# One unit for four PSUM score banks, and two delays in place of one in a list scheduler

## The chip, the cores and the metric

The kernel runs on one core of a Trainium2 chip. The metric is the device time of one execution in microseconds (us). A core has the matrix engine TensorE (PE; its weight loads are shown apart as PEld), VectorE (DVE), ScalarE (ACT), GpSimd (POOL) and SyncE (SP). SBUF is the working memory. PE writes its results into PSUM, which has eight banks of 128 partitions by 512 fp32 values.

## The reference

Four residual layers work on x of shape (4, 1024, 128), all in fp32. Each layer has an attention half and a feed-forward half, and both are modulated in the same way:

```python
h = _layernorm(x, axis=-1) * (1 + ca) + sa
x = x + ga * attn(h)
h = _layernorm(x, axis=-1) * (1 + cb) + sb
x = x + gb * ffn(h)
```

L0 is a decayed linear attention and a mixture of eight experts. L1 is a stack of four blocks of causal linear attention with 16 heads of 8 features, each block followed by two layer norms and a GELU network of 128 to 512 to 128, and then a mixture of eight experts. L2 and L3 are delta-rule attentions, each followed by one expert network that is picked per batch row. The change concerns the inside of L1's attention, which in each chunk of 128 steps computes

```python
scores = jnp.einsum('bnchd,bnkhd->bnhck', q, k)
scores = jnp.where(mask, scores, 0.0)
intra = jnp.einsum('bnhck,bnkhe->bnche', scores, v)
```

and adds to `intra` a part from the running state of earlier chunks, divided by a running denominator.

## The kernel before

x and h lie in SBUF with the 128 features on the partitions and 4096 tokens along the free axis. Each stage goes over eight chunks n of 128 steps and handles the four batch rows b of a chunk together, so a usual tile is 128 by 512.

**Two orderings stand behind each other.** The kernel writes its work as Python generators ("chains"): one for the normalisation, one for the scores, one for the masks, one for the value product and so on. The class `Flow` runs all the chains of one stage as a list scheduler. A chain yields what it wants next: `take` (buffers of a kind), `wait` (a mark that another chain sets), `rank` (its priority), or `run` (so many us on such engines). `Flow.run` keeps a planned clock for each engine. It goes on with the chain of best rank among those that can start within 0.1 us of the earliest. After a `run`, the chain's planned time is the end of the work plus the constant `LATENCY`, 0.12 us, for every engine alike (line 186). Buffers come free at the planned time of the chain that gives them back. When a chain goes on, it emits its instructions; the order of emission is a priority. A second scheduler, that of the framework, then sets the final order of each engine's instructions. It can put other ready work between instructions that one chain emitted together. The order of each engine is fixed before the kernel runs, and semaphores make an engine wait where its next instruction's data isn't there. No planned time appears on the chip.

The planner runs in five stages: `l0`, `l1_attn`, `l1_ffn`, `l2_attn` and `l3_attn`. The feed-forward halves of L2 and L3 are written straight out.

**L1's attention.** For each block l and chunk n, `prep_step` makes q, k, v, the denominators and `qx`, four copies of q masked by head (L966, on ACT). Then, for each batch row b (4 blocks x 8 chunks x 4 rows = 128 groups):

- `scores` takes four banks of the kind `sp` and issues four fp32 matmuls, one for each group d of 32 partitions, in the order d = 2, 3, 1, 0. Each contracts over 32 rows only, and the four use different rows of the PE array. The matmul helper records all of them as L291.
- `mask_dve` multiplies three of the banks (d = 0, 1, 2) by the causal mask on DVE (L1005) into SBUF tiles `at`, and then gives the three banks back.
- `mask_act` copies the fourth bank (d = 3) on ACT (L1018), gives it back, and masks the copy on POOL (L1021).
- `values` multiplies the masked scores with v in 16 small matmuls (L1080) into the bank of kind `acc`.

`attn_out` divides (L1096), applies the output projection and adds the residual (L1104); the chain `tail` does the norms and the GELU network (L1127, L1133). The norm's steps are L501 to L534: transposes on PE, a copy on ACT, statistics and scaling on DVE (L510 to L518), and a power on POOL (L515).

The eight PSUM banks of this stage are three `ps`, one `acc` and four `sp`. The four `sp` banks are in stock as single buffers: `take("sp", 4)` waits for all of them and hands them out in the order in which they came free, so a bank's role (d = 0 to 3) can change from group to group. Two of the four carry the profile's name ps and two the name acc.

Of the kernel before, what the change touches and what calls it, by code (L numbers as in the profile page):

```python
# [12 lines left out]
ALU = mybir.AluOpType  # L13
# [97 lines left out]
class Flow:  # L111
# [1 line left out]

    LATENCY = 0.12
    TABLE = 1.3
    SLACK = 0.1

# [35 lines left out]
    def run(self, chains):  # L155
        live = [{"gen": g, "t": 0.0, "want": None, "rank": 0.0, "no": i} for i, g in enumerate(chains)]
        while live:
            ready, asked = [], set()
            for c in sorted(live, key=lambda c: (c["rank"], c["no"])):
                if c["want"] is not None and c["want"][0] == "take":  # L160
                    kind = c["want"][1][0]
                    if kind in asked:
                        continue
                    asked.add(kind)
                s = self._start(c)
                if s is not None:
                    ready.append((s, c))
            assert ready, [c["want"] for c in live]
            first = min(s for s, _ in ready)
            at, c = next((s, c) for s, c in ready if s <= first + self.SLACK)  # L170
            got = None
            if c["want"] is None or c["want"][0] == "rank":
                self.at = c["t"]
            elif c["want"][0] == "spawn":
                self.at = c["t"]
                live.append({"gen": c["want"][1], "t": c["t"], "want": None, "rank": c["rank"], "no": c["no"]})
            elif c["want"][0] == "run":
                end = c["t"]
                table, costs = c["want"][1]
                if table and table != self.table:  # L180
                    self.table = table
                    self.clock["ACT"] += self.TABLE
                for e, cost in costs.items():
                    self.clock[e] = max(self.clock[e], c["t"]) + cost
                    end = max(end, self.clock[e])
                c["t"] = self.at = end + self.LATENCY
            elif c["want"][0] == "wait":
                c["t"] = self.at = at
            else:
                kind, n = c["want"][1]  # L190
                self.free[kind].sort(key=lambda b: b.free_at)
                got = [self.free[kind].pop(0) for _ in range(n)]
                c["t"] = self.at = at
            try:
                c["want"] = c["gen"].send(got)
                if c["want"][0] == "rank":
                    c["rank"] = c["want"][1]
            except StopIteration:
                live.remove(c)
# [6 lines left out]
def take(kind, n=1):  # L206
    return ("take", (kind, n))


def one(kind):  # L210
    (b,) = yield take(kind)
    return b


def rank(r):

    return ("rank", r)
# [7 lines left out]
def wait(key):  # L225
    return ("wait", key)


def mm_len(n, m=P):

    return max(n, m) * 0.00167 + 0.01


def dve_len(n):
    return 0.16 + 0.00104 * n


def act_len(n):
    return 0.25 + 0.00083 * n


def pool_len(n):
    return 0.2 + 0.0021 * n
# [6 lines left out]
def adaln_stack_kernel(ctx: ExitStack, tc: tile.TileContext, a):  # L250
    nc = tc.nc
    V, S, G, PE = nc.vector, nc.scalar, nc.gpsimd, nc.tensor
# [37 lines left out]
    def mm(out, lhsT, rhs, start=True, stop=True):  # L290
        PE.matmul(out, lhsT, rhs, start=start, stop=stop)  # L291

    def rep(ap, n):

        return ap.unsqueeze(1).to_broadcast([ap.shape[0], n, ap.shape[1]])
# [5 lines left out]
    def v4(t):  # L301
        return t.rearrange("p (a b) -> p a b", b=P)
# [11 lines left out]
    def K(name):  # L314
        lo, hi = _CONST[name]
        return cst[:, lo:hi]
# [9 lines left out]
    ident, mu, sl = K("ident"), K("mu"), K("sl")  # L326
# [148 lines left out]
    def flow():  # L475
        return Flow()

    def banks():
        return [ps() for _ in range(6)] + [acc() for _ in range(2)]
# [4 lines left out]
    def norm_stock(fl, n):  # L484

        fl.stock("xt", [v4(norm_tile(("ln_xc", "ln_sq", "ln_xn")[i % 3])) for i in range(n)])
        for kind, shape in (("st", (P, 4, 6)), ("mv", (P, 4, 2)), ("ve", (P, 4)), ("rs", (P, 4))):
            stock(fl, kind, 2, shape)
# [4 lines left out]
    def norm(fl, src, dst, affine):  # L493
# [3 lines left out]
        pb = yield from one("ps")  # L497
        p = v4(pb.t)
        yield run(PE=4 * TR_LEN)
        for t in range(4):  # L500
            PE.transpose(p[:, t, :], src[:, t, :], ident)  # L501
        xt = xb.t
        yield run(ACT=act_len(512))
        S.copy(xt, p)
        fl.give(pb)
        st, mv = (yield from one("st")), (yield from one("mv"))
        ve, rs = (yield from one("ve")), (yield from one("rs"))
        yield run(DVE=4 * dve_len(P) + 5 * 0.16)
        for t in range(4):
            V.bn_stats(st.t[:, t, :], xt[:, t, :])  # L510
# [330 lines left out]
    def l1_attn():  # L841
        y4 = h4
        fl = flow()
# [3 lines left out]
        psum = banks()  # L847
        fl.stock("ps", psum[:3])
        fl.stock("acc", psum[3:4])
        fl.stock("sp", psum[4:])  # L850
        norm_stock(fl, 3)
        fl.stock("z", [v4(norm_tile(tag)) for tag in ("ln_xc", "ln_sq", "ln_xn")])
        stock(fl, "qx", 2, (P, 4, B, P))
# [124 lines left out]
        ats, nums = {}, {}  # L978
        every = [(l, n) for l in range(L1L) for n in range(NS)]

        def scores():

            for l, n in every:
                yield rank(l * NS + n)
                yield wait(("prep", l, n))
                k, qx = ready[l, n][1].t, ready[l, n][5].t
                for b in range(B):
                    sps = yield take("sp", 4)
                    yield run(PE=mm_len(512) + 0.2)
                    for d in (2, 3, 1, 0):  # L990
                        g = slice(32 * d, 32 * d + 32)
                        mm(v4(sps[d].t), k[g, b, :], qx[g, :, b, :])
                    ats[l, n, b] = [sps, None, None]
                    fl.mark(("scores", l, n, b))

        def mask_dve():
            for l, n in every:
                yield rank(l * NS + n)
                for b in range(B):
                    yield wait(("scores", l, n, b))  # L1000
                    sps = ats[l, n, b][0]
                    at3 = yield take("at", 3)
                    yield run(DVE=3 * dve_len(512))
                    for d in range(3):
                        V.tensor_tensor(at3[d].t, v4(sps[d].t), rep(mu, 4), ALU.mult)  # L1005
                    fl.give(*sps[:3])
                    ats[l, n, b][1] = at3
                    fl.mark(("dve", l, n, b))

        def mask_act():  # L1010
            for l, n in every:
                yield rank(l * NS + n)
                for b in range(B):
                    yield wait(("scores", l, n, b))
                    sp = ats[l, n, b][0][3]
                    a = yield from one("at")
                    yield run(ACT=act_len(512))
                    S.copy(a.t, v4(sp.t))  # L1018
                    fl.give(sp)
                    yield run(POOL=pool_len(512))  # L1020
                    G.tensor_tensor(a.t, a.t, rep(mu, 4), ALU.mult)  # L1021
                    ats[l, n, b][2] = a
                    fl.mark(("act", l, n, b))
# [92 lines left out]
        def tail_step(l, n, z):  # L1116
# [22 lines left out]
            if l == L1L - 1:  # L1139
# [4 lines left out]
                fl.give(o)  # L1144

        chains = [attn_out(), state(), values(), mask_dve(), mask_act(), scores()]
        fl.run(chains + [tail(0), tail(1), prep(0), prep(1), first()])

# [699 lines left out]
    for i, half in enumerate([l0, l1_attn, l1_ffn, l2_attn, l2_ffn, l3_attn, l3_ffn]):  # L1848
        if half is l1_attn:
            early.close()  # L1850
        if half is l2_attn:
            late.close()
        with tc.tile_pool(name=f"half{i}", bufs=2) as wk:
            half()
# [99 lines left out]
```

## Time and profile before

| what | value |
|---|---|
| median of 3 runs | 2646.59 us (2646.0 to 2646.84) |
| the profiled execution | 2641.42 us |
| its span, first to last instruction | 2639.7 us |
| mean granted TensorE clock | 0.929 |
| PE busy | 2308.3 us (87%) |
| DVE busy | 1333.0 us (50%) |
| ACT busy | 1154.9 us (44%) |
| POOL busy | 892.2 us (34%) |
| chain that ended last | PE 64%, DVE 17%, ACT 7%, POOL 6% |

A group of instructions in the profile is named by line, engine, operation and tiles as out<-in, followed by shapes and count. Behind the bar stand busy time, the mean duration of one in ns, and the idle time of the engine just before them with what ended it. An fp32 matmul stands in the profile as two instructions, each with its own weight load, so the counts of matmuls are twice those of the code. In a view of the waits, "A <- B: 30.7, 26, 2.1" says that A's engine stood idle for 30.7 us in all, 26 times, 2.1 us at most, until B had finished. The clock is the share of full speed that the chip granted to PE.

### The profile page before, as it was taken

To read this page: it belongs to the slowest core of one execution; us is meant where nothing else is said; L and a number is where in the kernel's file an instruction comes from. 1 tells how busy PE (TensorE), PEld (TensorE's weight loads), DVE (VectorE), ACT (ScalarE), POOL (GpSimd) and SP (SyncE) were. 2 spreads that over 40 slices of the span, in tenths; PEclk is the share of its full clock that TensorE was granted. 3 is DMA by queue.
4 is the path that set the end of the run, shared out by engine and by line. 5 is a ranking of instruction groups with operands and counts; after the bars stand their busy time and mean duration, and the time that the engine had idled before them with its cause. 6 is when DMAs were issued, how large, how long until landed. Compare 5 with 4: busy or idle time off the path is not lost.

```text
span 2639.7 us, 36709 instructions
## 1 busy us (share of the span) xinstructions
PE 2308.3 (87%) x13822; PEld 1387.7 (53%) x13822; DVE 1333.0 (50%) x3930; ACT 1154.9 (44%) x1964; POOL 892.2 (34%) x885
## 2 busy tenths in 40 slices
PE   5999989899999988889899869999799878788966
PEld 4654445454545444444454434444789633687842
DVE  5764346664654556655665554343654224455422
ACT  3653245445545444444444333333544226545424
POOL 1334444332433333333333222333634001544400
PEclk9999989998999989999999888999899879899978
DMA  5323300000000000000000001110000000000001
GB/s 209 88 67 99 101 0 1 1 1 1 1 1 1 1 1 1 1 1 1 1 1 1 1 33 64 65 65 33 1 1 1 1 26 7 1 1 1 1 1 48
DMA packets 29010, 61.46 MB, mean 23 GB/s; under 512 B 4256, under 2 KB 4512, under 8 KB 27808
## 3 DMA queue, kind: packets, MB, share of 16 engines
q1 hardware_dynamic: 27072, 53.86, 6.3%
q0 software_dynamic: 896, 3.16, 0.4%
q8 instruction: 109, 1.79, 0.3%
q10 hardware_dynamic: 864, 2.09, 0.2%
q14 instruction: 69, 0.57, 0.1%
HBM read 56.74 MB, written 2.36 MB: 22 GB/s over the span
## 4 chain that ended last, share of the span: by engine, by line
PE 64%; DVE 17%; ACT 7%; POOL 6%; issue 3%; DMA 1%; SPq 0%; ACTq 0%; POOLq 0%; DVEq 0%
PE ps L291 38%; PE acc L291 15%; PE ps L1080 4%; POOL rs L515 2%; DVE at L1005 2%; DVE st L510 2%; PE ps L526 2%; PE ps L501 1%; DVE ln_sq L518 1%; POOL at L1021 1%; DVE ln_xc L518 1%; DVE ve L513 1%; PE ps L1258 1%; DVE x L455 1%; DVE ln_xn L518 1%
## 5 line engine op out<-in xcount | busy, mean ns | idle before, releaser
L291 PE MATMUL ps<-h,w 128*128 128x512 f32 x760 | 380.3, 616 | 33.3 <-DVE ln_xc L1104 8.7
L291 PEld LDWEIGHTS ps<-h,w 128*128 128x128 f32 x760 | 140.5, 197 | 191.1 <-issue 133.8
L1021 POOL TENSOR_TENSOR at<-at,cst 128x512 f32<-128x512 f32 x128 | 162.7, 1271 | 202.8 <-ACT at L1018 198.3
L291 PE MATMUL acc<-qx,k 32*128 32x512 f32 x512 | 209.7, 669 | 6.9 <-DVE at L1005 6.9
L291 PE MATMUL acc<-fu,w 128*128 128x512 f32 x432 | 210.6, 607 | 0.9 <-POOL fu L818 0.9
L515 POOL TENSOR_TENSOR rs<-ve,mhalf 128x4 f32<-128x4 f32 x120 | 122.9, 1024 | 252.6 <-DVE ve L513 230.1
L291 PE MATMUL ps<-qx,k 32*128 32x512 f32 x512 | 198.7, 671 | 7.2 <-DVE at L1005 7.2
L1080 PE MATMUL ps<-at,vz 128*32 128x128 f32 x4096 | 168.2, 292 | 36.8 <-POOL at L1021 30.7
L1235 POOL TENSOR_TENSOR lv<-cl,cst 128x512 f32<-128x512 f32 x112 | 141.2, 1273 | 164.0 <-PE ps L291 92.3
L1080 PEld LDWEIGHTS ps<-at,vz 128*32 128x32 f32 x4096 | 116.4, 116 | 111.7 <-issue 45.0
L1005 DVE TENSOR_TENSOR at<-acc,cst 128x512 f32<-128x512 f32 x190 | 126.9, 681 | 74.2 <-PE acc L291 46.1
L1005 DVE TENSOR_TENSOR at<-ps,cst 128x512 f32<-128x512 f32 x194 | 129.2, 680 | 56.6 <-PE acc L291 29.1
L1127 ACT ACTIVATE fu<-ps,cols 128x512 f32<-128x512 f32 x128 | 87.9, 687 | 156.3 <-PE ps L291 155.5
L818 POOL TENSOR_TENSOR fu<-fu,gate 128x512 f32<-128x512 f32 x88 | 110.9, 1266 | 131.0 <-DVE fu L814 114.9
L291 PE MATMUL ps<-fu,w 128*128 128x512 f32 x256 | 150.3, 672 | 5.3 <-ACT fu L1127 5.2
L291 PE MATMUL ps<-y,w 128*128 128x512 f32 x256 | 145.5, 652 | 8.5 <-DVE tmp L1040 2.1
L1203 ACT ACTIVATE fu<-ps,cols 128x512 f32<-128x512 f32 x128 | 88.0, 687 | 131.8 <-PE ps L291 128.5
L1207 POOL TENSOR_TENSOR fu<-fu,gate 128x512 f32<-128x512 f32 x64 | 83.4, 1310 | 166.7 <-ACT fu L1203 143.8
L291 PEld LDWEIGHTS acc<-fu,w 128*128 128x128 f32 x432 | 81.8, 195 | 95.2 <-issue 86.8
L1206 DVE TENSOR_TENSOR fu<-fu,gate 128x512 f32<-128x512 f32 x64 | 51.9, 823 | 119.7 <-ACT fu L1203 118.1
L291 PE MATMUL ps<-iU,lv 128*128 128x128 f32 x608 | 93.0, 301 | 20.4 <-DVE iU L1269 16.9
L291 PEld LDWEIGHTS ps<-iU,lv 128*128 128x128 f32 x608 | 83.2, 211 | 28.8 <-issue 12.1
(489 smaller groups left out, 4686.2 us busy)
## 6 DMA issues: line engine op xcount, KB each, us to landing
gate<-gd SPq DMA_DIRECT2D x96, 256.0 KB
w<-in_w SPq DMA_DIRECT2D x7, 1024.0 KB
gate<-gd SPq DMA_DIRECT2D x16, 224.0 KB
gate<-gd SPq DMA_DIRECT2D x16, 192.0 KB
gate<-gd SPq DMA_DIRECT2D x16, 160.0 KB
x<-in_x SPq DMA_DIRECT2D x8, 256.0 KB
gate<-gd SPq DMA_DIRECT2D x16, 128.0 KB
out_x<-x SPq DMA_DIRECT2D x8, 256.0 KB
```

What stands on the lines that cost most here:

```text
L291: PE.matmul(out, lhsT, rhs, start=start, stop=stop)
L510: V.bn_stats(st.t[:, t, :], xt[:, t, :])
L515: G.tensor_tensor(rs.t, ve.t, mhalf, ALU.pow)
L518: V.tensor_scalar(xt[:, t, :], xt[:, t, :], mv.t[:, t, 0:1], rs.t[:, t : t + 1], ALU.subtract, ALU.mult)
L818: G.tensor_tensor(u.t, u.t, g.t, ALU.mult)
L1005: V.tensor_tensor(at3[d].t, v4(sps[d].t), rep(mu, 4), ALU.mult)
L1021: G.tensor_tensor(a.t, a.t, rep(mu, 4), ALU.mult)
L1080: PE.matmul(num[g, b, :], vz[:, b, s * P + 32 * d : s * P + 32 * d + 32], at4[d].t[:, s, :], start=n == 0 and s == 0 and b == 0, stop=s == ...
L1127: S.activation(flat(u.t), pb.t, AF.Gelu, bias=C(f"l1_b1{l}", f))
L1203: S.activation(u.t, pa.t, AF.Relu, bias=C("l1f_b1", 2 * e + j))
L1207: G.tensor_tensor(us[1].t, us[1].t, g.t, ALU.mult)
L1235: G.tensor_tensor(b.t, cl.t, rep(lvl[:, k * P : (k + 1) * P], B), ALU.mult)
```

## The change

There are two parts.

In `Flow`, the delay behind a `run` is no longer 0.12 us for all. It becomes 0.10 us, and 0.16 us more when PE was among the engines of the `run`. This holds in all five planned stages.

In `l1_attn`, the four score banks become one unit. They are in stock as one buffer that holds a list of the four banks, so bank d always has role d. The unit is free again when both readers are through: the new function `through` notes the first and gives the unit back at the second. The planned cost of a score group grows by 0.1 us. Before the four score matmuls a matmul of one column is issued, which writes into one column of bank 3 from the rows 96 to 127 (d = 3); the full matmul of d = 3 overwrites that column later. No DMA is added, and the output is computed as before.

```diff
-    LATENCY = 0.12
+    LATENCY = 0.1
+    DRAIN = 0.16
...
-                c["t"] = self.at = end + self.LATENCY
+                c["t"] = self.at = end + self.LATENCY + (self.DRAIN if "PE" in costs else 0.0)
...
-        fl.stock("sp", psum[4:])
+        fl.stock("sp", [psum[4:]])
...
-                    sps = yield take("sp", 4)
-                    yield run(PE=mm_len(512) + 0.2)
+                    quad = yield from one("sp")
+                    yield run(PE=mm_len(512) + 0.3)
+
+
+                    mm(v4(quad.t[3])[:, 0, 0:1], k[96:, b, :], qx[96:, 0, b, 0:1])
                     for d in (2, 3, 1, 0):
                         g = slice(32 * d, 32 * d + 32)
-                        mm(v4(sps[d].t), k[g, b, :], qx[g, :, b, :])
-                    ats[l, n, b] = [sps, None, None]
+                        mm(v4(quad.t[d]), k[g, b, :], qx[g, :, b, :])
+                    ats[l, n, b] = [quad, None, None]
                     fl.mark(("scores", l, n, b))
+
+        def through(quad):
+
+            if half_read.pop(quad, None) is None:
+                half_read[quad] = fl.at
+                return
+            fl.give(quad)
+
+        half_read = {}
...
-                        V.tensor_tensor(at3[d].t, v4(sps[d].t), rep(mu, 4), ALU.mult)
-                    fl.give(*sps[:3])
+                        V.tensor_tensor(at3[d].t, v4(quad.t[d]), rep(mu, 4), ALU.mult)
+                    through(quad)
...
-                    S.copy(a.t, v4(sp.t))
-                    fl.give(sp)
+                    S.copy(a.t, v4(quad.t[3]))
+                    through(quad)
```

More of the change, by code (lines that the diff above doesn't have):

```diff
@@ L1000, in mask_dve @@
                     yield wait(("scores", l, n, b))
-                    sps = ats[l, n, b][0]
+                    quad = ats[l, n, b][0]
                     at3 = yield take("at", 3)
@@ L1014, in mask_act @@
                     yield wait(("scores", l, n, b))
-                    sp = ats[l, n, b][0][3]
+                    quad = ats[l, n, b][0]
                     a = yield from one("at")
                     yield run(ACT=act_len(512))
-                    S.copy(a.t, v4(sp.t))
-                    fl.give(sp)
+                    S.copy(a.t, v4(quad.t[3]))
+                    through(quad)
                     yield run(POOL=pool_len(512))
```

## The prediction

> **What bounds the kernel now.** I read the table by stretches first, cut where the stages begin and end.
>
> ```profile
> 45.00:366.00 321.00, 309.99 (x1144) 169.39 (x1142) 164.16 (x570) 134.02 (x255) 139.51 (x113) 0.99 0.25 73
> 366.00:1557.00 1191.00, 1060.96 (x7928) 567.09 (x7928) 693.98 (x1875) 550.04 (x830) 405.00 (x455) 0.93 0.00 1
> 1557.00:1840.00 283.00, 264.15 (x688) 119.37 (x688) 116.66 (x340) 110.64 (x189) 90.99 (x71) 0.95 0.18 60
> 1840.00:2077.00 237.00, 211.05 (x1628) 197.41 (x1628) 128.88 (x386) 107.05 (x249) 106.17 (x86) 0.94 0.00 1
> 2212.00:2510.00 298.00, 254.38 (x1795) 219.82 (x1794) 147.20 (x487) 156.77 (x294) 136.39 (x141) 0.93 0.00 1
> ```
>
> Columns: stretch and length, then busy time of PE, PEld, DVE, ACT, POOL, granted clock, DMA. The second row is the linear-attention stage: 1191 of 2640 us, PE busy for 1061 (89%), DVE 58%, ACT 46%, and no DMA. PE is the bound and is idle for 130 us. The other planned stages leave 11, 19, 26 and 44 us idle. So the change can gain by giving PE less to do or by taking PE's waits away. The timeline of PE in this stage shows the first:
>
> ```profile
> 1018.83 0.70 PE L291 MATMUL ps<-qx,k 32*128 32x512 f32 x2
> 1018.85 0.70 PE L291 MATMUL acc<-qx,k 32*128 32x512 f32 x2
> 1019.37 0.59 PE L291 MATMUL ps<-qx,k 32*128 32x512 f32 x2
> 1019.38 0.59 PE L291 MATMUL acc<-qx,k 32*128 32x512 f32 x2
> 1019.90 1.13 PE L291 MATMUL ps<-y,w 128*128 128x512 f32 x2
> ...
> 1024.57 1.12 PE L291 MATMUL acc<-qx,k 32*128 32x512 f32 x2
> 1025.62 1.13 PE L291 MATMUL ps<-fu,w 128*128 128x512 f32 x2
> 1026.67 0.69 PE L291 MATMUL ps<-qx,k 32*128 32x512 f32 x1
> ...
> 1039.57 0.96 PE L291 MATMUL ps<-cst,tmp 128*128 128x16 f32 x8
> 1040.38 0.64 PE L526 MATMUL ps<-cst,ln_sq 128*128 128x128 f32 x4
> ```
>
> Each fp32 matmul is two passes. Four score matmuls in four row groups run side by side: from 1018.83 to 1019.90, 1.07 us for all four. At 1024.57 one stands alone and takes 1.05 us as well, and its three partners come at 1026.67 for another 1.05. A divided group pays again for each part. The waits of PE in this stage show the second, the idle time:
>
> ```profile
> PE ps L1080 <- POOL at L1021: 30.7, 26, 2.1
> PE ps L291 <- DVE ln_xc L1104: 8.7, 5, 2.5
> PE ps L291 <- DVE ln_xn L1104: 8.7, 4, 2.5
> PE ps L291 <- DVE ln_sq L1104: 8.2, 4, 2.5
> PE ps L291 <- DVE at L1005: 7.2, 7, 3.8
> PE acc L291 <- DVE at L1005: 6.9, 13, 3.1
> PE ps L291 <- ACT fu L1127: 5.2, 8, 1.9
> ```
>
> The columns are total, times, longest. The masked scores that come over ACT and POOL are the largest (30.7); the bank that L1104 reads after the output projection holds up the next user three times over (25.6); the score banks cost 14.1.
>
> **The change, part by part.** The sum is made against the profiled execution (2641.4 us, span 2639.7); the median of the runs is 2646.6, and I carry the difference in us over to it. All counts of order come from the two built programs.
>
> *Score groups in one piece.* Before, the 128 groups lie in 212 stretches (58 groups whole, 48 as one and three). After, without the one-column matmuls, they lie in 191 (85 whole). 21 fewer x 1.05 us = **-22 us**, all on PE. The value matmuls (L1080), which use column groups, go from 156 stretches to 148; stretches of 8, 16, 24 and 32 passes take 0.36, 0.57, 0.79 and 1.01 us from start to start, so 0.14 us is the price of an extra one: **-1 us**.
>
> *The added matmul.* 128 matmuls of one column, two passes each, with two weight loads, in the row group of d=3, which then loads the same weights again. The trace has none. Nearest row: the 16-column matmuls at 1039.57, eight passes until 1040.38, 0.81/4 = 0.20 us each: 128 x 0.20 = 26 us. Looking inside a score stretch gives about the same: weights load in 0.107 us there (first load to second), and row group 3 gets two more loads before its own, 0.21 us, while the other three groups wait at the end for the slowest: 27 us. A rule speaks for less: the Trainium skill (TensorEngine Tiling, Instruction Overhead) has a matmul of one column cost about as much as one of 60, about 60 cycles. At the 128 columns per 0.107 us of this trace, 60 columns are 0.05 us, two passes 0.10, 128 of them 13 us. That leaves out the weight loads, which the row has in it, so I take **+27 us** and keep 13 for the range; the upper end is 0.30 us (0.21 plus a first load of 0.107 that nothing covers, where it stands apart from its group): 38. The two parts together are +4: the group in one piece pays for its own tie and no more. Another rule of the same page (Key Properties) is that a change of tiling mode drains the engine. The mode changes in this stage fall from 684 to 625, but the 1.05 us and 0.14 us above are start to start and have that in them, so I count nothing more.
>
> *The delays.* In the trace ACT starts 0.69 us (median) after the start of the last pass of a 128x512 matmul whose passes follow each other in 0.43 to 0.48: 0.21 to 0.26 behind PE, where the planner reckoned 0.12 and now 0.26. PE starts 0.05 us after DVE, ACT or POOL end, where it reckoned 0.12 and now 0.10. Both go towards the trace. A 512-column matmul is still planned at 0.865 us where the trace has 0.96. What it does is seen in the order alone. Laying PE's instructions end to end at the durations above, the room from the end of a group's scores to its first value matmul is under 2.3 us (0.1 + ACT 0.58 + 0.08 + POOL 1.27 + 0.05 and a little) in 33 groups before and in 19 after. 14/33 of the 30.7 us wait: **-13 us**. From one group's scores to the next the shortage against 2.3 us (three DVE reads of 0.68 and hand-offs) falls from 39 to 22 us in sum, 44% of the 14.1 us wait, -6. After the output projection the room until its bank is used again goes from 1.9 to 2.3 us at the median and from 2.0 to 3.7 at the upper quartile, against about 4.3 needed behind the normalisation's reads (L518) in DVE's queue; a third of 25.6 us, -8. PE is in order, and a wait gone often meets the next instruction's wait, so of these two I count half: **-7 us**. Bounds of all waits: -45 (twice what I count and a little) to +10.
>
> *Side effect on ACT.* The new order alternates more between exp (L895) and gelu (L1127): 36 table loads of each become 44.
>
> ```profile
> L895 ACT ACT_TABLE_LOAD x36 | 46.2, 1283 | 0.6
> L1127 ACT ACT_TABLE_LOAD x36 | 46.2, 1283 | 0.6
> ```
>
> 16 x 1.283 = 20.5 us of ACT. ACT is idle half of this stage, which is the cover; behind a load stand gelu and the mask copy (L1018), and PE waits for those. PE's waits for ACT are about 20 of its 130 us here, so I put a quarter on the path: **+5 us** (0 to 20.5 if the cover is gone).
>
> *The other flows* (L0, the first FFN, L2 and L3 attention) are replanned with the same instructions and DMAs, one table load apart at most. They have 100 us of PE idle; I take **-3**, within -12 to +10.
>
> Sum: -22 - 1 + 27 - 13 - 7 + 5 - 3 = **-14 us**, 2632 us at the median of runs.
>
> **The rivals.** *A, large gain:* the one-column matmul hides (13), the table loads are covered (0), the two halved waits count whole and L1104's twice over (-6, -16), and the other flows stand near their better end (-10): -22 - 1 + 13 - 13 - 6 - 16 - 10 = -55, 2592 us. For it: both delays move to what the trace shows. Against it: gelu's room from w1 to w2 shrinks at the upper quartile, from 3.0 to 2.3 us, and L1104 stays behind L518 in DVE's queue.
>
> *B, nothing:* tie against pieces, +4, and each wait replaced by another: about 2646.
>
> *C, slower:* ACT becomes the one that holds the score group. The one-column matmul stands at the head and waits for the bank that ACT frees at its copy; all of PE's queue stands behind it, and DVE and gelu wait for that. Before, no row of PE's waits names L1018, and the copy (0.58) is short against three DVE reads (2.04): that is against it. For it: four copies of 0.72 us (L966) in a row and 16 more table loads of 1.28 lie in ACT's queue. It decides from 14/128 = 0.11 us of extra wait per group on; at 0.22 us, some 22 groups caught behind one table load, +28: 2646.6 - 14 + 28 = 2660 us.
>
> **How the numbers follow.** Likeliest case 0.42, own range 2615 to 2641; A 0.18; B 0.12; C 0.28. Predicted 2632. The range runs from A's 2592 to a C with both the dear one-column matmul (+11) and no gain in the room, about 2670. Runs of one kernel lie within 0.03%, but I call 0.2% (5 us) the least that tells a change from none: faster 0.60, same 0.12, slower 0.28.
>
> **What would show it.** In the profile after: 128 more fp32 matmuls (256 passes) of 32 rows; DVE reads scores from ps 256 times and from acc 128 (now 194 and 190), and ACT's copy always from acc; 44 + 44 table loads. PE's busy time in the stage about level. The POOL wait of the value matmuls near 18 us, L1104's near 18. The start-to-start time of a whole group 1.28 rather than 1.07 us. A row of PE waiting for L1018's successor would speak for C. The prediction is wrong if the stage's length moves by more than some 25 us, or if the L2 and L3 attention stages move by more than 10.

## The result, and the profile after

The changed kernel takes 2615.9 us (median of 4 runs, 2611.5 to 2620.3) against 2646.3 us before: ratio 0.9888, 95% interval 0.9864 to 0.9912, or -30 us. The forecast was -14 us. The profiled execution of after took 2619.8 us with a span of 2618.0, which is 21.6 us under the span of before. The other 9 us are the spread of executions: the profiled one of before lies 4.9 us below its median, that of after 3.9 us above. The four runs of after come in two pairs, about 2620 us at a granted clock of 0.928 or 0.929 and about 2612 us at 0.933 or 0.934, and the profiled one is of the first pair.

The first thing to find out is in which stage the 21.6 us lie. The same instruction marks the end of each stage in both traces:

| from the span's start, us | before | after | moved |
|---|---|---|---|
| first score matmul of L1's attention | 384.3 | 384.3 | 0 |
| last score matmul | 1503.7 | 1471.6 | -32 |
| last y of L1's attention (L1133, now L1146) | 1537.8 | 1536.7 | -1 |
| last ReLU of L1's feed-forward half (L1203, now L1216) | 1836.1 | 1814.4 | -22 |
| end of L2 | 2204.2 | 2183.4 | -21 |
| end | 2639.7 | 2618.0 | -22 |

Nearly all of the prediction's working was about the attention stage, and that stage ends 1 us earlier. The whole gain of the profiled execution comes in the 280 us behind it, the mixture of experts, which the prediction had among the "other flows". Inside the attention stage something else is to be seen: the last score is 32 us earlier, and the stage's end is not. Part of that is the clock, as the experiments show.

The stretches of after, cut at its own stage ends (columns as before: PE, PEld, DVE, ACT, POOL busy, granted clock, DMA share and GB/s):

```profile
45.00:361.00 316.00, 306.99 (x1127) 167.59 (x1126) 162.13 (x542) 132.19 (x250) 132.24 (x108) 1.00 0.25 74
366.00:1557.00 1191.00, 1057.39 (x8197) 589.94 (x8198) 689.75 (x1902) 573.26 (x852) 409.12 (x459) 0.92 0.00 1
1557.00:1815.00 258.00, 253.47 (x672) 115.50 (x673) 109.30 (x335) 107.06 (x180) 88.17 (x71) 0.97 0.21 66
```

In the attention stage PE is as busy as before (1057 against 1061 us) in the same 1191 us. In the third row PE idles 4.5 of 258 us, where it idled 19 of 283, and the clock is 0.97 instead of 0.95.

The waits of PE in the attention stage, same view as before (total, times, longest):

```profile
PE ps L292 <- ACT fu L1140: 22.1, 24, 2.1
PE ps L1093 <- POOL at L1034: 19.9, 15, 2.9
PE ps L292 <- DVE ln_xc L1117: 4.4, 1, 4.4
PE acc L292 <- ACT at L1031: 1.7, 2, 0.9
PE acc L292 <- DVE at L1018: 1.5, 1, 1.5
```

The wait for POOL's masks is 19.9 (was 30.7). The bank behind the output projection (L1104, now L1117) is down from 25.6 to 5.8 us, with two small rows not shown; the score banks from 14.1 to 4.0, with one row of 0.8 not shown. In their place gelu (L1127, now L1140) stands at the top: 22.1 instead of 5.2. By engine, from the first score to the last y, PE's idle time behind DVE went from 56 to 36 us, behind POOL from 34 to 20, and behind ACT from 20 to 52. The sum is 110 before and 108 after.

PE's timeline shows a whole group with its one-column matmul, and the table loads of ACT follow:

```profile
1019.28 0.70 PE L292 MATMUL acc<-qx,k 32*128 32x1 f32 x2
1019.30 0.70 PE L292 MATMUL ps<-qx,k 32*128 32x512 f32 x2
1019.41 1.00 PE L292 MATMUL acc<-qx,k 32*128 32x1 f32 x3
1019.83 0.59 PE L292 MATMUL ps<-qx,k 32*128 32x512 f32 x2
1020.04 0.59 PE L292 MATMUL acc<-qx,k 32*128 32x512 f32 x1
1020.55 0.66 PE L911 MATMUL ps<-cst,k 128*128 128x128 f32 x4
```

```profile
L896 ACT ACT_TABLE_LOAD x44 | 56.5, 1283 | 0.8
L1140 ACT ACT_TABLE_LOAD x44 | 56.5, 1283 | 0.8
```

From 1019.28 to 1020.55 the group takes 1.27 us; the median of the whole groups is 1.274, against 1.071 before. (The row "x3" at 1019.41 joins the second one-column pass with the two passes of d=1.)

**Where the feed-forward gain comes from.** In each chunk the gates go through a chain of some twenty small DVE operations (from L572 to L557, in the function `route` and its helpers), then PE transposes them (L604). The DVE and POOL timeline of before at chunk 4:

```profile
1684.20 0.19 DVE L545 TENSOR_TENSOR rt<-rt,rm 128x32 f32<-128x32 f32 x1
1684.41 1.26 POOL L1207 TENSOR_TENSOR fu<-fu,gate 128x512 f32<-128x512 f32 x1 [6.52 <-ACT fu L1203]
1684.50 1.22 DVE L594 SCALAR_TENSOR_TENSOR rt<-rt 128x32 f32<-128x32 f32 x1
1686.54 0.68 DVE L1206 TENSOR_TENSOR fu<-fu,gate 128x512 f32<-128x512 f32 x1
1686.99 3.13 POOL L1207 TENSOR_TENSOR fu<-fu,gate 128x512 f32<-128x512 f32 x2 [1.31 <-ACT fu L1203]
1687.14 1.25 DVE L545 TENSOR_TENSOR rt<-rt,rm 128x32 f32<-128x32 f32 x1
1688.32 0.68 DVE L1206 TENSOR_TENSOR fu<-fu,gate 128x512 f32<-128x512 f32 x1
1688.92 1.25 DVE L596 TENSOR_TENSOR rt<-rt 128x32 f32<-128x32 f32 x1
1691.10 1.02 PE L604 MATMUL ps<-cst,rt 128*8 128x128 f32 x4 [3.26 <-DVE rt L557]
```

Two gate multiplies (L1206) stand inside the chain, and three 0.19-us operations take 1.22 to 1.25 us while POOL multiplies (L1207). Chain: 8.42 us, and PE stands for 3.26. What PE then runs, in windows of 4 us across that stall (clock is the third column from the end):

```profile
1684.00:1688.00 4.00, 3.84 (x9) 1.34 (x8) 3.72 (x9) 3.09 (x5) 2.28 (x2) 1.00 0.00 0
1688.00:1692.00 4.00, 0.90 (x5) 0.66 (x6) 2.91 (x7) 0.00 (x0) 2.11 (x2) 0.76 0.00 0
1692.00:1696.00 4.00, 4.00 (x6) 0.99 (x6) 0.00 (x0) 0.57 (x1) 0.00 (x0) 0.50 0.07 23
1696.00:1700.00 4.00, 4.00 (x5) 1.61 (x6) 0.00 (x0) 0.00 (x0) 0.00 (x0) 0.50 0.91 282
```

For the 8 us behind the stall PE is fully busy, with 5 or 6 passes in 4 us. The stall is paid a second time, as half speed. In after the chain of each chunk from the third on takes 4.8 to 5.4 us, with one gate multiply in it, and PE's gap before the transposes is 0 to 0.34. The waits of the stage, before and then after:

```profile
PE ps L604 <- DVE rt L557: 14.7, 7, 3.4
POOL fu L1207 <- DMA gate<-gd: 22.9, 4, 13.2
```

```profile
PE ps L605 <- DVE rt L558: 3.6, 3, 3.0
POOL fu L1220 <- DMA gate<-gd: 12.0, 5, 5.2
```

The stall gives back 11 us, and PE's idle time in the stage as a whole falls by 13.6 (18.1 to 4.5). The time at half clock falls from 26.3 to 13.7 us, worth half of the difference, or 6. Together that is the 20 us by which the stage got shorter (first ReLU to last, 274.0 to 253.7). POOL's wait for the DMA of the gates falls too, but it doesn't set the stage: the first run below has 4.6 us of it where after has 12.0, with the same stalls of PE.

### The profile page after: what moved, and what is told of

The parts are those of the page before. It is cut to its first block, busy times and chain, and to the rows that moved or that the text cites. A ratio compares the mean times of both kernels' runs of the same rounds, so it can differ in the third digit from the quotient of the medians.

```text
span 2618.0 us, 37183 instructions
## 1 busy us (share of the span) xinstructions
PE 2288.9 (87%) x14078; PEld 1400.5 (53%) x14078; DVE 1323.0 (51%) x3930; ACT 1174.5 (45%) x1980; POOL 890.0 (34%) x885
## 4 chain that ended last, share of the span: by engine, by line
PE 64%; DVE 15%; ACT 10%; POOL 5%; issue 3%; DMA 2%; SPq 0%; ACTq 0%; POOLq 0%; DVEq 0%
PE ps L292 36%; PE acc L292 17%; PE ps L1093 4%; POOL rs L516 3%; DVE st L511 2%; PE ps L527 2%; PE ps L502 1%; DVE at L1018 1%; ACT qx L967 1%; DVE ln_xc L519 1%; DVE ln_sq L519 1%; DVE ln_xn L519 1%; ACT L896 1%; PE ps L1271 1%; ACT fu L1140 1%
## 5 line engine op out<-in xcount | busy, mean ns | idle before, releaser
L292 PE MATMUL ps<-h,w 128*128 128x512 f32 x756 | 387.9, 625 | 14.9 <-ACT h L535 4.0
L292 PE MATMUL acc<-qx,k 32*128 32x512 f32 (+1 forms) x768 | 219.1, 528 | 7.3 <-POOL k L899 4.0
L1018 DVE TENSOR_TENSOR at<-ps,cst 128x512 f32<-128x512 f32 x256 | 166.7, 681 | 51.1 <-PE ps L292 49.2
L1093 PE MATMUL ps<-at,vz 128*32 128x128 f32 x4096 | 158.8, 284 | 26.7 <-POOL at L1034 19.9
L292 PE MATMUL ps<-qx,k 32*128 32x512 f32 x512 | 172.1, 656 | 0.9 <-DVE at L1018 0.8
L292 PE MATMUL ps<-fu,w 128*128 128x512 f32 x256 | 151.7, 676 | 22.2 <-ACT fu L1140 22.1
L819 POOL TENSOR_TENSOR fu<-fu,gate 128x512 f32<-128x512 f32 x88 | 111.1, 1267 | 132.0 <-DVE fu L815 100.9
L1140 ACT ACTIVATE fu<-ps,cols 128x512 f32<-128x512 f32 x128 | 87.9, 686 | 138.5 <-PE ps L292 137.9
L1216 ACT ACTIVATE fu<-ps,cols 128x512 f32<-128x512 f32 x128 | 88.0, 687 | 135.2 <-PE ps L292 131.2
L1018 DVE TENSOR_TENSOR at<-acc,cst 128x512 f32<-128x512 f32 x128 | 87.6, 685 | 86.6 <-PE ps L292 50.0
L1031 ACT COPY at<-acc 128x512 f32<-128x512 f32 x128 | 74.6, 582 | 119.6 <-PE acc L292 81.5
L292 PE MATMUL ps<-iU,lv 128*128 128x128 f32 x584 | 83.2, 287 | 28.2 <-DVE iU L1282 21.0
L292 PEld LDWEIGHTS acc<-qx,k 32*128 32x128 f32 x768 | 72.5, 190 | 63.2 <-issue 44.4
```

The costliest lines, as they stand in the source:

```text
L819: G.tensor_tensor(u.t, u.t, g.t, ALU.mult)
L1018: V.tensor_tensor(at3[d].t, v4(quad.t[d]), rep(mu, 4), ALU.mult)
L1031: S.copy(a.t, v4(quad.t[3]))
L1093: PE.matmul(num[g, b, :], vz[:, b, s * P + 32 * d : s * P + 32 * d + 32], at4[d].t[:, s, :], start=n == 0 and s == 0 and b == 0, stop=s == ...
L1140: S.activation(flat(u.t), pb.t, AF.Gelu, bias=C(f"l1_b1{l}", f))
L1216: S.activation(u.t, pa.t, AF.Relu, bias=C("l1f_b1", 2 * e + j))
```

## The experiments

The first theory was that the gain is the new delays at work in the feed-forward flow, and that the unit of banks brings nothing by itself; the rivals were that the unit, or the delays in the attention stage, bring it. Ratios are against the kernel before in the same series, with the 95% interval. "Attention end", "feed-forward end" and "end" are the movements of the three marks above in one profiled execution.

**The delays in the feed-forward flow alone.**

```diff
     LATENCY = 0.12
+    DRAIN = 0.0
...
-                c["t"] = self.at = end + self.LATENCY
+                c["t"] = self.at = end + self.LATENCY + (self.DRAIN if "PE" in costs else 0.0)
...
         fl = flow()
+        fl.LATENCY, fl.DRAIN = 0.1, 0.16
```

The last line stands in `l1_ffn` only.

> The kernel before with the two delays in the flow of L1's feed-forward stage alone. Theory 1: that stage goes from 274 to about 254 us between its first and last ReLU, nothing else moves: 2622 to 2630 us. Rival (the stage gains from where the attention stage leaves it, not from its own order): no gain, 2640 or more.

Measured 2618.8 us, 0.9902 (0.9885 to 0.9918). Attention end +0.1, feed-forward end -23.5, end -23.9. The chains of the gates are those of after. The waits of the stage:

```profile
PE ps L605 <- DVE rt L558: 3.7, 3, 3.0
POOL fu L1209 <- DMA gate<-gd: 4.6, 3, 2.0
```

Two constants in one flow, with the attention stage untouched, bring 26 of the 30 us. The first half of the theory stands.

**The delays everywhere, without the unit of banks.** Both constants and the line with `DRAIN`, as in the change; the score banks as before.

> The kernel before with the two delays alone; the four score banks stay single buffers and no one-column matmul is issued. The order of the built program has 185 score stretches (before 212, changed kernel 190) and 130 table loads. Theory 1 (the gain is the delays' effect on the order in L1's feed-forward stage; in the attention stage the unit's added matmul eats what fewer stretches save): the feed-forward stage is 20 us shorter than before as in the changed kernel, and the attention stage is shorter by 0.20 us x 91 groups = 18 us than in the changed kernel where that shows at its end; 2598 to 2620 us in all. Rival (the unit of four banks is needed for the gain): at most 10 us below before, 2636 or more.

Measured 2616.3 us, 0.9894 (0.9878 to 0.9911): within the interval of the whole change. Attention end -5.3, feed-forward end -29.0, end -26.6. So the unit of banks is not needed for the gain.

**The unit and the one-column matmul, with the old delays.**

```diff
-    LATENCY = 0.1
-    DRAIN = 0.16
+    LATENCY = 0.12
+    DRAIN = 0.0
```

> The changed kernel with the old delays: 0.12 us behind every engine. The unit, the added matmul and its cost stay. Theory 1: the feed-forward stage is as before and so is the attention stage, within 8 us; 2638 to 2655 us. Rival (the unit brings the gain): 2626 us or less.

Measured 2620.4 us, 0.9907 (0.9891 to 0.9924). Here the second half of the theory fell. The feed-forward stage has the order of before, with chains of 8.42 us, and took 2.6 us less, but the attention stage ended 15 us earlier, 6 of which it had at its first score. So each part alone gains about what both gain together; one of them must give something up when they meet. PE's waits in the attention stage:

```profile
PE ps L1093 <- POOL at L1034: 22.5, 19, 3.4
PE ps L292 <- ACT fu L1140: 8.7, 12, 1.7
```

The wait for gelu is 8.7 us with the unit alone, 14.5 with the delays alone, 22.1 with both.

**A longer planned cost for the gates.** The kernel before, with the chain's planned DVE time doubled:

```diff
             S.activation(ex.t, rest, AF.Exp)
-            yield run(DVE=2.4)
+            yield run(DVE=5.0)
```

> The kernel before, with the planned cost of the routing's run on DVE in that stage raised from 2.4 to 5.0 us; the delays and the banks are as before. Theory 1a (what counts is that the transposes of the gates don't stand on PE ahead of their data: each such stall of 3.3 us also halves the clock for up to 8 us): the three stalls of 3.3 us go and the stage gains 10 to 20 us, 2626 to 2637 us in all. Rival (the gain has another source, such as the delay behind PE for the expert chains): less than 5 us.

Measured 2638.5 us, 0.9971 (0.9959 to 0.9982); feed-forward end -4.1. The three stalls of 3.26 us stayed: the order still put two gate multiplies into the chain, and only the gaps of 0.53 us went. The edit did not do what it was meant to, so it says nothing on the theory except that the right cost of that step is not enough.

**Work for PE in the stall.** The kernel before, with three matmuls whose results nobody reads, ahead of the gate transposes of chunks 2, 4 and 6. If the half clock is a price of the idle time, the matmuls that follow should run at full clock.

```diff
         yield run(PE=4 * TR_LEN)
+        if bias is not None and n in (2, 4, 6):
+            for _ in range(3):
+                mm(pb.t, W(1, "fw1", 0), h[:, :512])
         for b in range(B):
```

> The kernel before, with three 512-column matmuls that nobody reads put on PE ahead of the gate transposes of chunks 2, 4 and 6 in L1's feed-forward stage (9 matmuls, 7.7 us of PE work), into the bank that the transposes then overwrite. These are the chunks where PE stands still for 3.26 us. If the stall itself is the price, the filler takes its place and nothing is gained: 2640 to 2647 us. If the stall also halves the granted clock behind it (in the trace of before 0.50 and 0.79 over the 8 us behind two of the three), the clock behind the transposes stays at 1.00 and the stage gets 4 to 7 us shorter although PE has more to do: 2636 to 2642 us.

Measured 2640.8 us, 0.9991 (0.9984 to 0.9997): less than expected. The windows of the same stall:

```profile
1684.00:1688.00 4.00, 4.00 (x11) 1.85 (x11) 3.40 (x13) 2.58 (x5) 1.26 (x1) 1.00 0.00 0
1688.00:1692.00 4.00, 3.04 (x8) 1.02 (x6) 3.93 (x7) 1.08 (x2) 3.12 (x2) 1.00 0.00 0
1692.00:1696.00 4.00, 3.42 (x11) 1.36 (x12) 0.46 (x3) 0.57 (x1) 0.00 (x0) 1.00 0.02 4
1696.00:1700.00 4.00, 4.00 (x10) 1.85 (x11) 0.00 (x0) 0.00 (x0) 0.00 (x0) 1.00 0.73 249
```

The gap fell from 3.26 to 1.54 us, and 10 passes stand where there were 5: the clock behind it is 1.00. The stage became 3.5 us shorter (274.0 to 270.5) though PE got 7.7 us more to do. By itself that is not clear of the spread: the unit with the old delays has this stage in the order of before and took 271.4.

The size of the second price is told by nine traces that have this stage in exactly the order of after. In each, PE stands for 2.98 to 3.03 us before the transposes of chunk 1. Behind that gap the clock stays full in two of them, is halved for 3.4 us in four and for 10.2 us in three. The stage takes 248.1 us in the first kind, 250.3 to 251.0 in the second and 253.5 to 253.7 in the third. The same instructions in after (third kind) and in the unit without the one-column matmul (first kind, below):

```profile
1560.00:1815.00 255.00, 250.47 (x666) 113.65 (x665) 107.78 (x327) 105.69 (x179) 88.17 (x71) 0.97 0.21 67
```

```profile
1553.00:1802.00 249.00, 244.01 (x666) 111.22 (x665) 107.49 (x327) 105.23 (x178) 88.00 (x71) 1.00 0.21 68
```

So one such stall cost, beside its length, nothing, 2 to 3 us or 5.5 us, with the same instructions.

**The change without the one-column matmul.**

```diff
-                    mm(v4(quad.t[3])[:, 0, 0:1], k[96:, b, :], qx[96:, 0, b, 0:1])
                     for d in (2, 3, 1, 0):
```

> The changed kernel without the one-column matmul; the unit, its planned cost and the delays stay. 191 score stretches against 190. If the added matmul costs what the trace of the changed kernel shows (1.274 against 1.071 us in 85 whole groups, 17 to 19 us) and PE's work sets the attention stage's end: that stage ends 12 to 19 us earlier, 2597 to 2606 us. If the end of the stage is set by the chain of its last tails: within 5 us of the changed kernel, 2611 to 2621 us.

Measured 2607.6 us, 0.9862 (0.9846 to 0.9879). That is 8 us under the change, or 5 us when each is taken against the kernel before in its own series, and the intervals overlap. The one-column matmul does not hold the groups together: they stay in 191 stretches without it (192 with it). In the profiled execution the attention stage is 16 us shorter (1136.1 against 1152.4), but begins 8.4 us later.

**The unit, with the new delays in the feed-forward flow only.** The edit is that of the unit with the old delays, and `fl.LATENCY, fl.DRAIN = 0.1, 0.16` in `l1_ffn`.

> The unit with its added matmul everywhere with the old delays, and the new delays in L1's feed-forward stage alone. If the two single gains are of different stages (attention -15 us by the unit alone, feed-forward -24 us by the delays alone) they add up: 2645 - 15 - 6 - 24, 2597 to 2607 us. If what the one gains the other gives back wherever they stand together, as in the changed kernel: 2612 to 2620 us.

Measured 2607.3 us, 0.9868 (0.9851 to 0.9885); attention end -9.5, feed-forward end -29.9, end -32.9. So with the unit there, the new delays outside the feed-forward half seem to cost 5 to 9 us, but the interval overlaps that of the change, so this is not shown. The same without the one-column matmul:

> The unit without the added one-column matmul, old delays everywhere but in L1's feed-forward stage: 196 score stretches, 140 table loads. Against the same with the added matmul (2607 us): the tie cost 8 us between the changed kernel and the one without it. If that holds here too: 2594 to 2602 us, the fastest so far. If the tie had held the groups together at run time: 2607 or more.

Measured 2598.7 us, 0.9832 (0.9816 to 0.9849). That matmul costs 7 to 9 us here, and the two intervals are apart.

**The delays in both flows of L1, without the unit.** `fl.LATENCY, fl.DRAIN = 0.1, 0.16` in `l1_attn` and `l1_ffn`.

> The delays in the two flows of L1 alone, single banks, no added matmul; L0, L2 and L3 are planned as before. With the delays everywhere L0 ended 7.8 us later and L2's attention took 4 to 5 us longer than before; without that the gain of the delays alone, 29 us, grows to 37 to 42 us: 2603 to 2609 us. If the attention stage doesn't start from where L0 leaves it with the same order: anything from 2603 to 2620.

Measured 2620.6 us, 0.9922 (0.9905 to 0.9938); attention end +2.0, feed-forward end -21.6. A miss. The order inside the attention stage is that of the delays everywhere, yet from the first score to the last y it took 1153.1 us against 1140.4 there. The two as rows of the stretches, the delays everywhere first:

```profile
392.00:1532.00 1140.00, 1010.33 (x7861) 544.44 (x7860) 675.87 (x1810) 549.52 (x813) 394.21 (x443) 0.95 0.00 1
```

```profile
387.00:1540.00 1153.00, 1023.59 (x7861) 551.87 (x7861) 676.97 (x1810) 550.31 (x815) 394.79 (x444) 0.93 0.00 1
```

PE has the same instructions, all but a few in the same order, and its idle time differs by 1 us; its busy time is 13 us longer, at a lower clock. So this stage has to be split before it is compared. When each busy microsecond of PE at half clock is counted as half of one of work, the time from the first score to the last y is:

| us | work | lost to half clock | PE idle | sum |
|---|---|---|---|---|
| before | 976.5 | 66.0 | 111.1 | 1153.6 |
| after | 965.3 | 76.6 | 110.5 | 1152.4 |
| after without the one-column matmul | 949.6 | 75.0 | 111.6 | 1136.1 |
| delays everywhere, no unit | 951.8 | 58.4 | 130.2 | 1140.4 |
| delays in L1, no unit | 950.0 | 73.8 | 129.4 | 1153.1 |

One order can lose 15 us more to the clock in one execution than in another, though four traces with the order of before all lose 66 or 67. The change takes 11 us of work from PE, nothing from its waits in sum, and the profiled execution of after lost 11 us more to the clock than that of before. Whether the order has a part in this loss is open.

**Without the table loads.** The exponential of q and k is replaced by a ReLU, in the kernel before and in the changed one, so the result is another; 71 and 87 table loads leave the stage.

```diff
             for e in es:
-                S.activation(e.t, e.t, AF.Exp)
+                S.activation(e.t, e.t, AF.Relu)
```

> The kernel before with ReLU in the place of exp in L1's attention (the output is not the reference's), so that ACT needs no table load there (71 of them leave, 91 us of ACT); the planner still plans as if they were there. The second scheduler moves PE's order too: 183 score stretches in place of 212, worth 30 us. PE's waits for ACT in the stage were 19.7 us with the loads. If loads reach PE only through ACT, these fall below 10 us, and the stage is 30 to 45 us shorter than before: 2600 to 2616 us.

> The changed kernel with the same replacement (87 loads leave, output not the reference's); 171 score stretches in place of 190, worth 20 us. PE's waits for ACT in the stage were 52.0 us. Theory 2 (the added ACT waits of the changed kernel come from its table loads): they fall below 20 us, and the stage is 45 to 60 us shorter than in the changed kernel, so more than before without loads: 2556 to 2572 us. Rival (they come from the order alone, gelu's chain planned too tight): more than 35 us of ACT waits stay and the stage is about 20 to 30 us shorter: 2587 to 2597 us.

Measured 2583.8 us, 0.9781 (0.9753 to 0.9808) for before, and 2566.7 us, 0.9716 (0.9696 to 0.9735) for after. From the first score to the last y, before goes from 1153.6 to 1106.4 us and after from 1152.4 to 1105.2: 47 us in each. There are two runs of each. Before gains more than expected, and after as much as expected. But the two 47 are not made of the same parts, because the replacement also moves the order: the score stretches fall by 29 in before (212 to 183) and by 19 in after (190 to 171). PE's work falls by 29 and 12 us, its idle time by 7 and 19, the loss to the clock by 11 and 16. PE's idle time behind ACT falls from 20 to 14 us in before and from 52 to 26 in after. So 20 of the 32 us by which after waits longer behind ACT go with the loads, and 12 stay. That speaks against the order alone, but as the order moves too it doesn't show what the 16 added loads cost. In after, the wait for gelu falls from 22.1 to 5.7:

```profile
PE ps L527 <- DVE ln_xc L519: 17.8, 7, 5.1
PE ps L1093 <- POOL at L1034: 13.9, 17, 2.4
PE ps L292 <- ACT fu L1140: 5.7, 12, 0.8
```

**The rank of the tail.** Where in the attention stage the gain is given back is seen when each profile is cut at the last score:

| us | first to last score | last score to last y | sum |
|---|---|---|---|
| before | 1119.4 | 34.2 | 1153.6 |
| after | 1087.3 | 65.1 | 1152.4 |
| delays everywhere, no unit | 1090.4 | 50.0 | 1140.4 |
| unit, old delays | 1090.9 | 53.2 | 1144.1 |
| after without the one-column matmul | 1071.2 | 64.9 | 1136.1 |
| before without table loads | 1072.3 | 34.1 | 1106.4 |
| after without table loads | 1039.8 | 65.4 | 1105.2 |

Each part of the change, and both together, gain some 29 us or more up to the last score, and lose 16 to 31 of them behind it. Not all of this is gain and loss, for work moves across the cut: behind the last score after has 15 us more of PE's work than before, 11 us more of idle time and 4 us more lost to the clock. The table loads, taken away, gain 47 us ahead of the cut and nothing behind it. The tail of before and that of after, as rows of the stretches:

```profile
1515.00:1538.00 23.00, 19.42 (x60) 8.22 (x60) 11.86 (x57) 9.86 (x15) 4.03 (x4) 1.00 0.00 1
```

```profile
1482.00:1537.00 55.00, 39.03 (x110) 17.73 (x109) 23.11 (x110) 18.28 (x28) 8.08 (x8) 0.84 0.00 0
```

Before, 23 us of norms and GELU network are left behind the last residual (L1104), PE is idle for 3.6 of them and the clock is 1.00. After, 55 us are left, PE is idle for 16 and the clock is 0.84. The scores ran ahead: four tails end behind the last score where two did, and nothing is left there to fill PE's waits with. The planner decides this by one constant: `tail` asks for rank `l * NS + n + behind`, one chunk later than its own scores. In the version with the unit, without the one-column matmul and with the new delays in the feed-forward flow only:

```diff
-        ahead, behind = -3, 1
+        ahead, behind = -3, 0
```

> As the run beside it (unit, no added matmul, new delays in the feed-forward stage alone), with the rank of the tail chains one chunk earlier (behind = 0 in place of 1): 188 stretches, 136 loads. In the changed kernel the last scores end 33 us earlier than before but the last tail no earlier. If the tails at the end set the stage's end, it ends 5 to 15 us earlier than in the run beside it: 2582 to 2595 us. If PE's work and waits in the middle set it: within 6 us of it.

Measured 2574.5 us, 0.9742 (0.9725 to 0.9758), against 0.9832 for the same version with `behind = 1`. From first to last score it takes 1085.8 us (1089.4 with 1), behind it 35.6 us (53.6). So 18 us of the difference lie behind the last score. About 10 of them are PE's work that has moved ahead of it, and the part ahead does not grow by it, because PE's idle time falls there by 8 us. In the stage as a whole PE idles 11 us less and loses 9 less to the clock. The order of the middle changed as well (188 score stretches for 196), so not all of this need come from the tail. What is left behind the last residual, with `behind = 1` and with 0:

```profile
1490.00:1529.00 39.00, 30.82 (x93) 13.93 (x91) 19.50 (x94) 15.99 (x24) 6.04 (x6) 0.87 0.00 0
```

```profile
1484.00:1506.00 22.00, 18.29 (x58) 7.97 (x56) 10.79 (x50) 8.57 (x13) 3.02 (x3) 1.00 0.00 0
```

The last 22 us look like those of before: 3.7 us idle, clock 1.00. This is the fastest version with the reference's output, 2.6% under the kernel before.

## Why the prediction was wrong

The direction was right, and 2615.9 us lies in the range, at the lower edge of the likeliest case's own (2615 to 2641). The cause was not: -11 us were put on the attention stage and -3 on the others; in the profiled execution it was -1 and -21.

**The step that failed is the term of the other flows (-3, within -12 to +10).** "Replanned with the same instructions" was taken to mean little. L1's feed-forward flow alone gave 20 us in the profile, and its two constants alone 26 of the 30 us between the medians. The trace of before held 14.7 us of stalls in one row (L604), at one place per chunk, with half clock behind three of the four that were over 3 us. There the delays decide whether one or two multiplies fall into the chain of the gates. L2's attention took 1 us longer and L3's 2 us less, within the bound given.

**Score groups in one piece (-22, and -1 for the values): held.** 212 stretches became 192, two of which hold a one-column matmul alone.

**The one-column matmul (+27): too high.** Of the 128, 36 stand in front of a d=2 score alone, and such a stretch takes 1.058 us where a lone score takes 1.051: row group 3 has nothing else to do there. In the 85 whole groups it costs 1.274 - 1.071 = 0.203 us, as worked out from the 0.20-us row. 85 x 0.203 + 36 x 0.007 is 17.5 us, and some for the seven others; without that matmul PE's work in the stage is 15.7 us less. The medians have 5 to 9 us. The 13 us by the skill's rule (TensorEngine Tiling, Instruction Overhead) is not right either: where nothing covers it, the trace has the 0.2 of the row, with the weight loads in it.

**The wait for POOL's masks (-13): held**, -10.8. **The score banks and the bank behind the output projection (-7 together): too low.** They fell by 10 and 20 us. But from these three rows, -41 us in all, PE's idle time in the stage gained 0.6 us: gelu's row rose by 17, those behind rb (L960), q (L887) and y (L1146) by 6 to 8 each, and others by less. The prediction had 15 us of waits gone, after +5 for ACT. The caution that a wait gone often meets the next one was right, and should have held for all of them; that was rival B's step.

**The side effect on ACT (+5): the term was mis-sized.** 44 + 44 loads came, as said. Waits behind ACT rose by 32 us. Without loads the two kernels differ by 12 us in these waits, so loads and order both seem to have a part. From the two built orders the prediction had read that gelu's room shrinks at the upper quartile from 3.0 to 2.3 us, and used it only as an argument against rival A.

**The sum for the attention stage (-11) came out by luck.** It was +4 of work and -15 of waits. Work and idle time together fell by 11.8 us, but as 11.2 of work and 0.6 of waits, and 10.6 more were lost to the clock, for which the prediction had no term.

**A step that the prediction did not have:** it took time saved between scores as time by which the stage ends earlier. The stage ends with its last tail, and in the new order what lies behind the last score is 31 us longer. The trace of before showed a short tail (34 us) and the new order was at hand, so it could have been counted. The run with `behind = 0` shows that the tail's rank is worth 24 us in the version tried; it was not run on the changed kernel itself.

**The rivals.** A's steps for the two bank waits came true, but not its sum. C did not: the row of PE waiting for ACT's copy is 1.7 us. The mark that the prediction set for itself, a stage that moves by no more than 25 us, was met, but only because 32 us ahead of the last score and 31 behind it cancelled.

**Open.** Up to the last score each part alone gains 29 us, and both together 32. The longer tail may be one reason that they don't add, the gelu waits and the clock others; none was tried apart. The 5 to 9 us that the new delays seem to cost outside the feed-forward half, when the unit is there, lie within the spread of single profiles and were not traced to a place.

## What to carry to other kernels

A planner's constant changes every flow that it orders: for each, look for the row of waits that repeats at the same place in every chunk, and count it as a candidate for the largest gain, before working on the stage that the change is about. Cut a stage at the last start of its main work: time saved ahead of that cut is no gain until the work behind it also ends earlier, and some of it may be work that has moved across. Before two profiles of one execution are compared, take out what each lost to the clock. And in a stage that PE bounds, a stall of about 3 us costs its length and then up to 5.5 us more for matmuls at half speed, differently in each execution.

## What the runs showed of the hardware

**The clock is granted in whole pieces.** The spells of low clock behind the stalls in the feed-forward stage of before are 3.4 and 10.2 us long, and in the rest of the traces nearly all are 3.4, 6.8, 10.2, 13.7 and more, at 0.50. The Trainium skill (TensorE: Matmul & The Clock Gate, Part 1) has half clock after an idle window of about 3.4 us that runs freely. The spells agree in length; but less idle time was enough here: a gap of 2.98 us in after (chunk 1) was followed by a clock of 0.51 over the next 8 us, and the three gaps of 3.26 or 3.27 in before by 0.79, 0.50 and 1.00. With gaps of 1.54 us it stayed at 1.00 behind all three. Over four traces, twelve gaps of 3.25 to 3.27 us were followed by no half clock three times, by 3.4 us six times and by 10.2 us three times.

**A small DVE operation can wait for a whole POOL instruction.** 0.19 us became 1.22 to 1.25 us beside POOL multiplies of 1.26 us and more (L545, L594, L596 above). Over the kernel before, 142 DVE operations took over 0.3 us more than the median of their line and shape, 118 us together, 48 of them the norm's scaling (L518) with 44 us. Which ones is a matter of where they read: of the operations that started while POOL multiplied, those with both inputs in SBUF were stretched (L545 to 1.24 at least; a residual that reads SBUF alone, L455, to 1.34 and more in eight of ten cases), and so were many of the scalings with one input there. The mask multiplies (L1005), with one input in PSUM, kept to 0.66 to 0.69 us in all 89 cases, and the statistics (L510, L512) to 0.14 to 0.30. The skill (SBUF — State Buffer, Who interferes with whom) draws the same line.

**A part of a group of row tiles costs like the whole.** One, two, three or four score matmuls in their row groups take 1.051, 1.058, 1.065 and 1.071 us.
